# Two more chunks of the MLP's first product inside the last attention slots, in place of zero matmuls, and the rows of two batches transposed earlier

## The chip, the cores and the metric

The kernel runs on one core of a Trainium2 chip. The core has a matrix engine (TensorE, called PE in the profile; its weight loads are shown as PEld), a vector engine (VectorE, DVE), an activation engine (ScalarE, ACT), a general engine (GpSimd, POOL) and a queue engine that issues the transfers (SyncE, SP). Each engine runs its own instructions in order and waits for others by semaphores. The metric is the device time of one execution in microseconds; the median of several runs is compared.

## The reference

One transformer block with two attentions and an MLP, in float32: 16 batches of 256 tokens with 256 features, 16 heads of 16.

```python
x_norm = modulate(_ln(x), shift_a, scale_a)
qkv = x_norm @ W_qkv + b_qkv                       # self-attention, 16 heads
x = x + gate_a[:, None] * (softmax(q k^T * scale) v @ W_proj + b_proj)
q_c = _ln(x) @ W_qc + b_qc                         # attention to the context
kv_c = _ln(context) @ W_kvc + b_kvc
x = x + (softmax(q_c k_c^T * scale) v_c @ W_cproj + b_cproj)
x_norm2 = modulate(_ln(x), shift_m, scale_m)
h = jax.nn.gelu(x_norm2 @ W_mlp1 + b_mlp1)         # 256 -> 1024
x = x + gate_m[:, None] * (h @ W_mlp2 + b_mlp2)    # 1024 -> 256
```

(The two softmax lines are shortened.) The change lies in the MLP: `x_norm2 @ W_mlp1` is called the first product here, `h @ W_mlp2` the second product.

## The kernel before, in words

**Precision.** Float32 products are made of three products of a faster type: each matrix is split into a high part and a low remainder, and high times high, high times low and low times high are summed in PSUM (`mm3`, `mm3_tok`).

**Slots and beats.** There are 32 attention units: 16 of self-attention ("s") and 16 of attention to the context ("c"), in one order, `units`. The last four units, 28 to 31, are all "c" (batches 12 to 15). A loop runs over slots n = -1 to 31, and each slot over eight beats k = 0 to 7 (`beat(n, k)`). In a beat PE makes the scores of unit n+1 from which DVE takes the row maxima (tile `s`, maxima `mx`), and the transposed scores of unit n (tile `st`), which ACT turns into exponentials (`pt`). In beats 0 and 4 the maxima are transposed (`psm`) and sent by SP as a row (`m`) into the stacked queries `big`, and PE multiplies exponentials and values (`o`, 32 instructions). The rest of a beat is other work of neighbouring units: transposing `o` (`psA`, beats 2 and 6), dividing by the sums (`norm`, DVE, tiles `rc` and `A`), transposing again (`psT_a`, beat 4), the output projection (`psP`, beat 6 of the last slots) and, for earlier slots, the projections of units to come. In slots 30 and 31 there are no units to come, so there is less for PE to do; some of the gaps are filled with matmuls of zeros (`busy`, tile `ps_warm`; the words `d2` and `d3` in the table `SL` are two and three of them).

**The tail.** After slot 31 the MLP of all 16 batches runs, in 64 chunks: four chunks per batch, each of 256 hidden features. A chunk is a first product (12 matmuls into one PSUM bank, tile `ph`, `mlp_first`), two gelus on ACT from the same input (`hf` in full float32, `hh` rounded), their difference on POOL (`hl`, `mlp_gelu`) and a second product (12 matmuls, `mlp_second`, accumulated in the tile `s` or `st`). Iteration i of the tail issues the gelu of chunk i+1, the first product of chunk i+2, and the second product of chunk i-1. A batch b also needs: its rows loaded from DRAM (`mlp_load`, SP, tile `x`), a bias added (`mlp_bias`, POOL), layer-norm statistics (`mlp_stats`, DVE, with a power on POOL, `rs_m`), the normalised rows (`mlp_apply`, DVE, `xn_m`), and their transposes, scaled and split into high and low (`mlp_T`: PE `psT_m`, then DVE `xTf_m`, then `wkch` or `wqch`, then DVE `wkcl` or `wqcl`; these tiles were the context weights before). In the tail the bias, the statistics and `xn_m` of batch b+2 are issued in the iteration of chunk 1 of batch b, and the transposes of batch b+1 in that of chunk 0 of batch b.

**Already inside the slots.** For batches 0, 1 and 2 these steps are issued in the attention slots, at the positions in the table `M`. A position p means slot p // 16 + 31 and beat (p mod 16) // 2, after the beat's own work: -17 is the end of beat 7 of slot 29, 1 is beat 0 of slot 31. The four first products of batch 0 are issued in slot 31 as well (table `H`), and since their gelu comes only in the tail (the activation table is changed once), they are parked: DVE adds the bias of the hidden features and copies the bank into a tile in SBUF (`hk`). The tail then begins with the first products of chunks 4 and 5.

**Order.** The order on PE, DVE, POOL and SP is the order of the program (class `InOrder`); on ACT too, up to iteration 23 of the tail.

**PSUM.** Two tags of two banks each are handed out in turn: "gen" (`LONG`) and "tr" (`SHORT`); a new tile waits until the last reader of the tile two before it in its tag is done. In slot 30 the odd beats' scores use "gen". The tags of SBUF tiles that park chunks are `c` (two buffers), `x1` (five) and, after the change, `xg` (two).

**Weights of the MLP.** They are loaded and split inside slots 23 to 31 (`W1P`, `W2P`): the last two pieces of the first product's weights are split in beats 3 and 5 of slot 29, and those of the second product in beats 2, 4 and 6 of slot 30 and beat 0 of slot 31. The loads of `x` rows and of the second product's weights (`w2_0` to `w2_3`, in slots 28 and 29) share five buffers in turn.

Of the kernel before, what the change touches and what calls it, by code (L numbers as in the profile page):

```python
# [21 lines left out]
def pixart_block(  # L22
# [8 lines left out]
    B, N, H = x.shape  # L31
# [20 lines left out]
                return tc.keep_in_program_order(i) if self.on else i  # L52
            return issue

    E_ = {'M': ((-17, -12, -10, -1, 1), (0, 3, 4, 7, 9), (8, 11, 13, 15)), 'CUT': 8, 'LN': {'s': 'pool', 'c': 'pool', 'q': 'pool'}, 'ON': (1, 1, 1), 'L0': -16, 'L1': 1, 'S0': -7, 'A0': 0, 'T0': 1, 'H': (7, 11, 14, 15), 'S1': 5, 'A1': 7, 'L2': 9, 'T1': 9, 'S2': 32, 'AP': 23, 'DV': (0, 1), 'HP': (1, 0), 'BZ': {}, 'AV': {1: [(1, 2), (1, 3)], 9: [(0, 0), (0, 1)]}, 'AHEAD': (0, 0, 0, 0, 0, 2), 'W1P': [(-9, 1), (-8, 1), (-7, 1), (-6, 1), (-5, 1), (-5, 5), (-4, 1), (-4, 3), (-4, 5), (-3, 1), (-3, 3), (-3, 5), (-2, 1)], 'W2P': [(-4, 7), (-3, 0), (-3, 4), (-3, 6), (-3, 7), (-2, 2), (-2, 4), (-2, 6), (-1, 0), (-1, 1)], 'XP': 1, 'IL': 1, 'MF': 0, 'SH': 4, 'RAMP': 1, 'HA': 1, 'MP': 16, 'W': (7, 1, 0, 0), 'PRE': 'z0qp z0kp load rest ld2 one0 silu b12 brow L0a turn L0b b4 L0d scale T0t sc1 hik lok T0h T0l b4 shift b4 hiq L1a L1b bk loq K0a K0b K0x0 K0x1 K0y0p K0y1p L1d T1t K0l T1h K0l0 K0l1 Q0a Q0m bq Q0h Q0x0 Q0y0p Q0x1 Q0y1p T1l Q0l Q0l0 Q0l1 z1kp z1qp K1a K1b hiv lov Q1a Q1b K1x0 K1x1 K1y0 K1y1 K1l K1l0 K1l1 Q1x0 Q1x1 Q1y0 Q1y1 Q1l Q1l0 Q1l1 L2a L2b L2c V0a V0b bv b5 ld3', 'SL': {(-1, 0): 'V1a', (-1, 1): 'T2t T2h T2p vone z2kp z2qp', (-1, 2): 'V1b', (-1, 3): 'rest', (-1,4): 'M0 rest one1 ld4', (-1, 5): 'K2a L3a', (-1, 6): 'K2m L3b L3p L3c', (-1, 7): 'd3 one2 rest', (0, 0): 'd6 rest', (0, 1): 'rest', (0, 2): 'd3', (0, 4): 'rest', (1, 0): 'rest', (1, 2): 'rest', (1, 4): 'rest', (30, 0): 'd3', (30, 1): 'd2', (30, 2): 'd3', (30, 5): 'd3', (31, 1): 'd2'}}

    PE = InOrder(nc.tensor, True)
    ACT, DVE, POOL, SP = (InOrder(e, True) for e in (nc.scalar, nc.vector, nc.gpsimd, nc.sync))
# [6 lines left out]
    LONG, SHORT = "gen", "tr"  # L65
    ps_turn = [0]

    def ps_gen(name, tag=None):


        if tag is None and ps_turn[0] is not None:
            ps_turn[0] ^= 1
            tag = (SHORT, LONG)[ps_turn[0]]
        tag = tag or SHORT
        return psum.tile([P, 512], F32, tag=tag, name=name, bufs=2)
# [29 lines left out]
    brow = const.tile([32, P], F32, name="brow")  # L105
# [8 lines left out]
    def split(hi, lo, src, eng=POOL, hp=0):  # L114
        (DVE, POOL, ACT)[E_['HP'][hp]].tensor_copy(hi, src) if E_['HP'][hp] < 2 else ACT.copy(hi, src)
        eng.tensor_tensor(lo, src, hi, ALU.subtract)
# [9 lines left out]
    sc1 = const.tile([P, 2, 2, B], F32, name="sc1")  # L126
# [142 lines left out]
    def layernorm(src, name):  # L269
# [83 lines left out]
    def mm3(dst, W, f, xT):  # L353

        n = 0
        for k in range(KC):
            for a, b in ((W[0], xT[0]), (W[0], xT[1]), (W[1], xT[0])):
                PE.matmul(dst, a[:, k, f * P:(f + 1) * P], b[:, k],
                          start=(n == 0), stop=(n == 3 * KC - 1))
                n += 1  # L360
# [335 lines left out]
    M = {}  # L696
# [8 lines left out]
    def mlp_bias(b):  # L705
        POOL.tensor_tensor(M[b].xt, M[b].xt, bc_t(cb), ALU.add)
# [16 lines left out]
    def mlp_T(b):  # L723
# [9 lines left out]
        for f in range(KC):  # L733
            DVE.tensor_scalar(y[:, f], pst[:, f * N:(f + 1) * N], sc1[:, 1, f, b:b + 1],
                              cpT[:, 6 + f, b:b + 1], ALU.mult, ALU.add)
        if b in E_['DV']:
            DVE.tensor_copy(hi, y)
# [6 lines left out]

    NCH = NF // 2

    def mlp_first(b, c, park=None):

        ph = ps_gen(f"ph_{b}_{c}", LONG).rearrange("p (j n) -> p j n", j=2)
        for j in range(2):  # L750
            mm3(ph[:, j], W1, 2 * c + j, M[b].xT)
        if park is not None:
            kept = work.tile([P, 2, N], F32, tag=park[0], name=f"hk_{b}_{c}", bufs=park[1])
            for j in range(2):
                f = BM1 + 2 * c + j
                DVE.tensor_scalar(kept[:, j], ph[:, j], bT[:, f:f + 1], None, ALU.add)
            ph = kept
        M[b].h[c] = ph

    def mlp_gelu(b, c):  # L760
        ph = M[b].h.pop(c)
        hf = work.tile([P, 2, N], F32, tag="pt", name=f"hf_{b}_{c}", bufs=5)
        hh = work.tile([P, 2, N], F32R, tag="qkh", name=f"hh_{b}_{c}", bufs=3)
        hl = work.tile([P, 2, N], F32R, tag="qkl", name=f"hl_{b}_{c}", bufs=3)
        for dst in (hf, hh):
            if b == 0:
                ACT.activation(dst, ph, AF.Gelu_apprx_tanh)
                continue
            for j in range(2):
                f = BM1 + 2 * c + j  # L770
                ACT.activation(dst[:, j], ph[:, j], AF.Gelu_apprx_tanh, bias=bT[:, f:f + 1])
        POOL.tensor_tensor(hl, hf, hh, ALU.subtract)
        M[b].hT[c] = (hh, hl)
# [17 lines left out]

    W1P, W2P = E_['W1P'], E_['W2P']
    W1 = [wself[:, 8 * i:8 * i + 8].rearrange("p (k c) h -> p k (c h)", k=KC) for i in range(2)]
    W2 = [big[2][:, 0], big[2][:, 1]]

    def mlp_w1():

        wf = []
        SP.dma_start(cb, cd[0].partition_broadcast(P))
        for j in range(4):  # L800
            wf.append(stage(W_mlp1, j * H, f"w1_{j}", "x"))
            yield
# [56 lines left out]
    w1, w2, rest = mlp_w1(), mlp_w2(), setup_rest()  # L859
# [58 lines left out]
    for i in range(3):  # L918
        for n, f in (("b", f_b), ("hi", f_hi), ("lo", f_lo)):
            word[n + "qkv"[i]] = lambda f=f, i=i: f(i)  # L920
    for w in E_['PRE'].split():
        word[w]()
    for p, ws in E_['SL'].items():
        at[p] += [word[w] for w in ws.split()]
    ACT.on, POOL.on, SP.on = E_['ON']
    at_end = defaultdict(list)
    def end(p, f, *a):
        at_end[p // 16 - 1, p % 16].append(lambda: f(*a))

    for b, ps in enumerate(E_['M']):  # L930
        for p, f in zip(ps, (mlp_load, mlp_bias, mlp_stats, mlp_apply, mlp_T)):
            end(p, f, b)
    for c, p in enumerate(E_['H']):
        end(p, mlp_first, 0, c, (("c", 2), ("x1", 5))[c // 2])
    def unit(n):
        return units[n] if 0 <= n < nu else None

# [176 lines left out]
                lambda: (o.aT.turn(), o.aT.high()), o.aT.low,  # L1114
                lambda: o.proj(0), lambda: o.proj(1), lambda: (o.end(), o.add(), o.store())])
    chunks = [(b, c) for b in range(B) for c in range(NCH)]
    mlp_first(*chunks[4])
    mlp_gelu(*chunks[0])
    next(pst)()
    mlp_first(*chunks[5])  # L1120
    next(pst)()
    for i, (b, c) in enumerate(chunks):
        ACT.on = i < E_['AP']
        if i + 1 < len(chunks):
            mlp_gelu(*chunks[i + 1])
        if c == 0 and 0 < b < B - 1:
            mlp_T(b + 1)
        if i > 3 and i + 2 < len(chunks):
            mlp_first(*chunks[i + 2])
        if i > 0:  # L1130
            mlp_second(*chunks[i - 1])
        for _, f in zip(range(1), pst):
            f()
        if c == 1 and 2 < b + 2 < B:
            mlp_bias(b + 2)
            mlp_stats(b + 2)
            mlp_apply(b + 2)
        if c == 2:
            mlp_residual(b)
        if c == 3 and b + 3 < B:  # L1140
            mlp_load(b + 3)
# [49 lines left out]
```

## Time and profile before

| | us |
|---|---|
| median of 3 runs | 805.61 |
| lowest and highest | 803.01 and 806.17 |
| the profiled execution | 804.78 |
| its span, first to last instruction | 803.0 |

The span is the time between the first and the last instruction that the profile shows; 1.78 us of the profiled execution lie around it. In the timeline an instruction row gives start, length, engine, line, operation, output and inputs, and in brackets the idle time of the engine before it with what ended it. Lengths of matmuls overlap since they are pipelined; the cost of a group is better read from its start to the start of the next group. All kernel lines carry L51, the line of the helper that issues every instruction, so that rows are told apart by their tiles. Slot 30 lies from 566.9 us on, slot 31 from 586.8 to 607.0, the tail after that.

### The profile page before, as it was taken

How to read it: one execution, taken by the hardware profiler on the slowest of the kernel's cores; microseconds unless marked ns; L12 is line 12 of the kernel's file. 1: busy time of each engine (PE TensorE's matmuls, PEld its weight loads, DVE VectorE, ACT ScalarE, POOL GpSimd, SP SyncE). 2: the span in 40 equal slices, each digit the busy share in tenths (PEclk: the TensorE clock that was granted, in tenths of full speed). 3: DMA queues.
4: the chain of work that ended last, by engine and by line, in shares of the span. 5: the costliest groups of instructions: out<-in, count | busy, mean ns of one | idle time of the engine just before them, and what ended most of it. 6: DMA issues, size and time to landing. Idle time of an engine off the chain costs nothing.

```text
span 803.0 us, 23712 instructions
## 1 busy us (share of the span) xinstructions
PE 781.8 (97%) x9455; PEld 660.3 (82%) x9455; DVE 596.0 (74%) x1063; ACT 584.8 (73%) x1024; POOL 465.4 (58%) x405
## 2 busy tenths in 40 slices
PE   9999999999999999999999999999899999999997
PEld 8677777887887877878788788777669999999997
DVE  4787878888888888878887888777674656666662
ACT  3377887888887888878888788877666666666663
POOL 5745837475564647456364767654446666666653
PEclk9999999999999999999999999999999999999999
DMA  6553444345353444535444454534311322212211
GB/s 189 147 172 95 133 113 123 100 120 146 95 147 104 137 107 123 146 94 146 113 132 130 137 151 120 148 101 129 106 42 42 92 60 60 80 58 62 80 43 51
DMA packets 89938, 87.88 MB, mean 109 GB/s; under 512 B 9506, under 2 KB 85572, under 8 KB 89828
## 3 DMA queue, kind: packets, MB, share of 16 engines
q1 hardware_dynamic: 89364, 85.58, 37.7%
q8 instruction: 75, 1.23, 0.7%
q0 software_dynamic: 192, 0.52, 0.2%
q14 instruction: 35, 0.29, 0.1%
q10 hardware_dynamic: 272, 0.26, 0.1%
HBM read 26.97 MB, written 8.46 MB: 44 GB/s over the span
## 4 chain that ended last, share of the span: by engine, by line
PE 79%; DVE 9%; ACT 4%; POOL 3%; issue 3%; DMA 1%; ACTq 0%; POOLq 0%; SPq 0%
PE s L51 17%; PE o L51 14%; PE ph L51 11%; PE st L51 11%; DVE mx L51 7%; PE ps_qc L51 3%; PE ps_kc L51 3%; PE ps_q L51 3%; ACT pt L51 2%; PE ps_P_s L51 2%; PE ps_v_s L51 2%; PE ps_v_c L51 2%; PE psm L51 2%; PE ps_k L51 1%; PE ps_P_c L51 1%
## 5 line engine op out<-in xcount | busy, mean ns | idle before, releaser
L51 DVE TENSOR_REDUCE mx<-s 128x4 f32<-128x1024 f32 (+1 forms) x267 | 309.2, 1163 | 94.6 <-PE s L51 92.0
L51 ACT ACTIVATE pt<-st 128x1024 f32<-128x1024 f32 x252 | 257.0, 1020 | 40.3 <-PE st L51 34.1
L51 PE MATMUL s<-big 63*128 63x256 f32 (+1 forms) x1024 | 122.1, 309 | 6.5 <-DVE mx L51 3.6
L51 PE MATMUL o<-pt,v 128*32 128x256 f32 x2048 | 123.8, 382 | 0.0
L51 POOL TENSOR_TENSOR hl<-hf,hh 128x512 fp32r<-128x512 f32 x64 | 88.7, 1396 | 55.0 <-ACT hh L51 54.0
L51 PEld LDWEIGHTS s<-big 63*128 63x128 f32 (+1 forms) x1024 | 81.2, 185 | 41.6 <-DVE mx L51 19.0
L51 PE MATMUL st<-big 64*128 64x256 f32 (+1 forms) x1024 | 108.8, 284 | 4.9 <-ACT pt L51 4.9
L51 PEld LDWEIGHTS o<-pt,v 128*32 128x32 f32 x2048 | 60.0, 109 | 40.8
L51 PEld LDWEIGHTS st<-big 64*128 64x128 f32 (+1 forms) x1024 | 82.1, 186 | 9.3 <-ACT pt L51 7.5
L51 ACT ACTIVATE hf<-ph,bT 128x256 f32<-128x256 f32 x120 | 50.6, 474 | 27.8 <-PE ph L51 27.8
L51 ACT COPY oT<-o 128x512 f32<-128x512 f32 x63 | 37.0, 587 | 42.5 <-PE o L51 42.5
L51 ACT ACTIVATE hh<-ph,bT 128x256 fp32r<-128x256 f32 x120 | 50.5, 472 | 23.8 <-PE s L51 12.0
L51 POOL TENSOR_TENSOR xTl_c<-y_c,xTh_c 128x512 fp32r<-128x512 f32 x16 | 20.5, 1282 | 61.6 <-PE s L51 52.3
L51 POOL TENSOR_TENSOR xTl_as<-y_as,xTh_as 128x512 fp32r<-128x512 f32 x16 | 20.5, 1279 | 56.4 <-ACT y_as L51 56.4
L51 PE MATMUL ph<-wqch,wself 128*128 128x256 f32 x256 | 51.8, 285 | 0.0
L51 PE MATMUL ph<-wkch,wself 128*128 128x256 f32 x256 | 51.8, 286 | 0.0
L51 POOL TENSOR_TENSOR xTl_ac<-y_ac,xTh_ac 128x512 fp32r<-128x512 f32 x16 | 20.6, 1284 | 52.8 <-ACT y_ac L51 48.8
L51 PE MATMUL s<-big,hh 128*128 128x256 f32 x256 | 47.4, 282 | 0.0
L51 PE MATMUL st<-big,hh 128*128 128x256 f32 x256 | 47.2, 281 | 0.0
L51 DVE TENSOR_SCALAR xn_m<-x,mv_m,rs_m 128x256 f32<-128x256 f32 x32 | 38.4, 1238 | 11.4 <-POOL rs_m L51 11.4
L51 PEld LDWEIGHTS ph<-wqch,wself 128*128 128x128 f32 x256 | 42.0, 191 | 0.4 <-issue 0.4
L51 PEld LDWEIGHTS ph<-wkch,wself 128*128 128x128 f32 x256 | 41.9, 191 | 0.4
(223 smaller groups left out, 2381.0 us busy)
## 6 DMA issues: line engine op xcount, KB each, us to landing
big<-h_kc SPq DMA_DIRECT2D x64, 128.0 KB
big<-h_qc SPq DMA_DIRECT2D x64, 128.0 KB
big<-h_k SPq DMA_DIRECT2D x62, 128.0 KB
big<-h_q SPq DMA_DIRECT2D x62, 128.0 KB
big<-l_k SPq DMA_DIRECT2D x32, 128.0 KB
big<-l_q SPq DMA_DIRECT2D x32, 128.0 KB
c<-in_ctx_dram SPq DMA_DIRECT2D x16, 256.0 KB
g<-gd SPq DMA_DIRECT2D x16, 256.0 KB
```

The source lines that it names most:

```text
L51: i = f(*a, **k)
```

## The change

The four first products in slot 31 become six first products in slots 30 and 31: chunks 0 and 1 of batch 0 are issued in beats 3 and 5 of slot 30 (into "tr" banks), chunks 2 and 3 in beats 1 and 3 of slot 31, and chunks 0 and 1 of batch 1 in beats 5 and 7 of slot 31. All six are parked. The zeros of beat 5 of slot 30 (three) and of beat 1 of slot 31 (two) go; those of beats 0, 1 and 2 of slot 30 stay. So that the rows are there, all steps of batches 0 and 1 move:

| step | batch 0 before | batch 0 after | batch 1 before | batch 1 after |
|---|---|---|---|---|
| load | slot 29 beat 7 | slot 29 beat 1 | slot 31 beat 0 | slot 30 beat 2 |
| bias | slot 30 beat 2 | slot 29 beat 2 | slot 31 beat 1 | slot 30 beat 4 |
| statistics | slot 30 beat 3 | slot 29 beat 3 | slot 31 beat 2 | slot 30 beat 6 |
| normalised rows | slot 30 beat 7 | slot 29 beat 6 | slot 31 beat 3 | slot 31 beat 0 |
| transposes | slot 31 beat 0 | slot 30 beat 1 | slot 31 beat 4 | slot 31 beat 1 |

Batch 2's positions stay. The tail begins with the first products of chunks 6 and 7, and iterations 4 and 5 issue none (before: iterations 0 to 3 none). The gelus of the two parked chunks of batch 1 are issued as one instruction of 512 columns each instead of two of 256 with a bias.

```diff
-'M': ((-17, -12, -10, -1, 1), (0, 3, 4, 7, 9), (8, 11, 13, 15))
+'HT': 'tr', 'M': ((-30, -28, -25, -20, -14), (-11, -7, -3, 0, 2), (8, 11, 13, 15))
...
-'H': (7, 11, 14, 15)
+'H': ((-9, 0, 0, 'x1', 5), (-5, 0, 1, 'xg', 2), (3, 0, 2, 'x1', 5), (7, 0, 3, 'c', 2), (11, 1, 0, 'c', 2), (15, 1, 1, 'xg', 2))
...
-(30, 0): 'd3', (30, 1): 'd2', (30, 2): 'd3', (30, 5): 'd3', (31, 1): 'd2'
+(30, 0): 'd3', (30, 1): 'd2', (30, 2): 'd3'
...
-    def mlp_first(b, c, park=None):
-        ph = ps_gen(f"ph_{b}_{c}", LONG).rearrange("p (j n) -> p j n", j=2)
+    def mlp_first(b, c, park=None, tag=LONG):
+        ph = ps_gen(f"ph_{b}_{c}", tag).rearrange("p (j n) -> p j n", j=2)
...
-            if b == 0:
+            if b == 0 or b == 1 and c < 2:
                 ACT.activation(dst, ph, AF.Gelu_apprx_tanh)
...
-    for c, p in enumerate(E_['H']):
-        end(p, mlp_first, 0, c, (("c", 2), ("x1", 5))[c // 2])
+    for p, b, c, *park in E_['H']:
+        end(p, mlp_first, b, c, park or None, E_['HT'] if p < 0 else LONG)
...
-    mlp_first(*chunks[4])
+    mlp_first(*chunks[6])
...
-    mlp_first(*chunks[5])
+    mlp_first(*chunks[7])
...
-        if i > 3 and i + 2 < len(chunks):
+        if i > 5 and i + 2 < len(chunks):
             mlp_first(*chunks[i + 2])
```

More of the change, by code (lines that the diff above doesn't have):

```diff
@@ L53, in __getattr__ @@
             return issue
-    E_ = {'M': ((-17, -12, -10, -1, 1), (0, 3, 4, 7, 9), (8, 11, 13, 15)), 'CUT': 8, 'LN': {'s': 'pool', 'c': 'pool', 'q': 'pool'}, 'ON': (1, 1, 1), 'L0': -16, 'L1': 1, 'S0': -7, 'A0': 0, 'T0': 1, 'H': (7, 11, 14, 15), 'S1': 5, 'A1': 7, 'L2': 9, 'T1': 9, 'S2': 32, 'AP': 23, 'DV': (0, 1), 'HP': (1, 0), 'BZ': {}, 'AV': {1: [(1, 2), (1, 3)], 9: [(0, 0), (0, 1)]}, 'AHEAD': (0, 0, 0, 0, 0, 2), 'W1P': [(-9, 1), (-8, 1), (-7, 1), (-6, 1), (-5, 1), (-5, 5), (-4, 1), (-4, 3), (-4, 5), (-3, 1), (-3, 3), (-3, 5), (-2, 1)], 'W2P': [(-4, 7), (-3, 0), (-3, 4), (-3, 6), (-3, 7), (-2, 2), (-2, 4), (-2, 6), (-1, 0), (-1, 1)], 'XP': 1, 'IL': 1, 'MF': 0, 'SH': 4, 'RAMP': 1, 'HA': 1, 'MP': 16, 'W': (7, 1, 0, 0), 'PRE': 'z0qp z0kp load rest ld2 one0 silu b12 brow L0a turn L0b b4 L0d scale T0t sc1 hik lok T0h T0l b4 shift b4 hiq L1a L1b bk loq K0a K0b K0x0 K0x1 K0y0p K0y1p L1d T1t K0l T1h K0l0 K0l1 Q0a Q0m bq Q0h Q0x0 Q0y0p Q0x1 Q0y1p T1l Q0l Q0l0 Q0l1 z1kp z1qp K1a K1b hiv lov Q1a Q1b K1x0 K1x1 K1y0 K1y1 K1l K1l0 K1l1 Q1x0 Q1x1 Q1y0 Q1y1 Q1l Q1l0 Q1l1 L2a L2b L2c V0a V0b bv b5 ld3', 'SL': {(-1, 0): 'V1a', (-1, 1): 'T2t T2h T2p vone z2kp z2qp', (-1, 2): 'V1b', (-1, 3): 'rest', (-1,4): 'M0 rest one1 ld4', (-1, 5): 'K2a L3a', (-1, 6): 'K2m L3b L3p L3c', (-1, 7): 'd3 one2 rest', (0, 0): 'd6 rest', (0, 1): 'rest', (0, 2): 'd3', (0, 4): 'rest', (1, 0): 'rest', (1, 2): 'rest', (1, 4): 'rest', (30, 0): 'd3', (30, 1): 'd2', (30, 2): 'd3', (30, 5): 'd3', (31, 1): 'd2'}}
@@ new lines, in pixart_block @@
+    E_ = {'HT': 'tr', 'M': ((-30, -28, -25, -20, -14), (-11, -7, -3, 0, 2), (8, 11, 13, 15)), 'CUT': 8, 'LN': {'s': 'pool', 'c': 'pool', 'q': 'pool'}, 'ON': (1, 1, 1), 'L0': -16, 'L1': 1, 'S0': -7, 'A0': 0, 'T0': 1, 'H': ((-9, 0, 0, 'x1', 5), (-5, 0, 1, 'xg', 2), (3, 0, 2, 'x1', 5), (7, 0, 3, 'c', 2), (11, 1, 0, 'c', 2), (15, 1, 1, 'xg', 2)), 'S1': 5, 'A1': 7, 'L2': 9, 'T1': 9, 'S2': 32, 'AP': 23, 'DV': (0, 1), 'HP': (1, 0), 'BZ': {}, 'AV': {1: [(1, 2), (1, 3)], 9: [(0, 0), (0, 1)]}, 'AHEAD': (0, 0, 0, 0, 0, 2), 'W1P': [(-9, 1), (-8, 1), (-7, 1), (-6, 1), (-5, 1), (-5, 5), (-4, 1), (-4, 3), (-4, 5), (-3, 1), (-3, 3), (-3, 5), (-2, 1)], 'W2P': [(-4, 7), (-3, 0), (-3, 4), (-3, 6), (-3, 7), (-2, 2), (-2, 4), (-2, 6), (-1, 0), (-1, 1)], 'XP': 1, 'IL': 1, 'MF': 0, 'SH': 4, 'RAMP': 1, 'HA': 1, 'MP': 16, 'W': (7, 1, 0, 0), 'PRE': 'z0qp z0kp load rest ld2 one0 silu b12 brow L0a turn L0b b4 L0d scale T0t sc1 hik lok T0h T0l b4 shift b4 hiq L1a L1b bk loq K0a K0b K0x0 K0x1 K0y0p K0y1p L1d T1t K0l T1h K0l0 K0l1 Q0a Q0m bq Q0h Q0x0 Q0y0p Q0x1 Q0y1p T1l Q0l Q0l0 Q0l1 z1kp z1qp K1a K1b hiv lov Q1a Q1b K1x0 K1x1 K1y0 K1y1 K1l K1l0 K1l1 Q1x0 Q1x1 Q1y0 Q1y1 Q1l Q1l0 Q1l1 L2a L2b L2c V0a V0b bv b5 ld3', 'SL': {(-1, 0): 'V1a', (-1, 1): 'T2t T2h T2p vone z2kp z2qp', (-1, 2): 'V1b', (-1, 3): 'rest', (-1,4): 'M0 rest one1 ld4', (-1, 5): 'K2a L3a', (-1, 6): 'K2m L3b L3p L3c', (-1, 7): 'd3 one2 rest', (0, 0): 'd6 rest', (0, 1): 'rest', (0, 2): 'd3', (0, 4): 'rest', (1, 0): 'rest', (1, 2): 'rest', (1, 4): 'rest', (30, 0): 'd3', (30, 1): 'd2', (30, 2): 'd3'}}
```

## The prediction

> **What bounds the kernel now.** I read the page first (busy shares, slices), then the busy time by stage around the change, then the chain of waits, then the timeline of slots 30 and 31 engine by engine. TensorE (PE) is the bound everywhere; the question is where it has gaps.
>
> ```profile
> PE 781.8 (97%) x9455; PEld 660.3 (82%) x9455; DVE 596.0 (74%) x1063; ACT 584.8 (73%) x1024; POOL 465.4 (58%) x405
> ```
>
> By stage (window, its length, then busy us of PE, PEld, DVE, ACT, POOL, granted clock, DMA share, GB/s). The rows are slot 30, slot 31, the head of the tail up to batch 2's transposes, from these to batch 3's, and the rest:
>
> ```profile
> 569.30:587.40 18.10, 15.89 (x173) 11.68 (x165) 13.03 (x27) 11.14 (x15) 9.08 (x9) 1.00 0.21 63
> 587.40:607.00 19.60, 19.34 (x181) 14.33 (x181) 14.11 (x36) 12.35 (x16) 8.95 (x8) 1.00 0.14 43
> 607.00:618.50 11.50, 11.50 (x113) 10.54 (x113) 3.36 (x8) 7.82 (x17) 6.45 (x7) 1.00 0.21 71
> 618.50:630.90 12.40, 12.19 (x104) 11.96 (x102) 7.22 (x14) 8.06 (x20) 9.77 (x8) 1.00 0.32 87
> 630.90:797.00 166.10, 166.10 (x1376) 163.66 (x1377) 97.17 (x180) 102.68 (x244) 100.04 (x79) 1.00 0.21 63
> ```
>
> Slot 30 has 2.2 us without a matmul, slot 31 0.3, the tail only 0.21, at the transposes of batch 3. The reader should see two things: zeros are PE time too (a slot with zeros is full without being useful), and the tail has no slack, so a chunk that leaves it should be worth its 1.43 us. The chain of waits in the tail (start, length) says otherwise:
>
> ```profile
> 618.66 0.44 PE psT_m L51 x4
> 619.10 1.43 PE ph L51 x12
> 620.53 1.43 PE s L51 x12
> 621.97 1.45 PE ph L51 x12
> 623.41 1.49 POOL hl L51
> 624.90 1.25 POOL x L51
> 626.16 1.25 issue
> 627.45 0.70 POOL rs_m L51
> 628.15 0.03 issue
> 628.18 2.67 DVE xn_m L51 x2
> 630.85 0.04 issue
> 630.89 0.55 PE psT_m L51 x3
> ```
>
> Between the transposes of batch 2 (618.50) and of batch 3 (630.89) PE does not set the end: batch 3's bias, statistics and normalising do, 12.3 us after batch 2's transposes. PE fills that time exactly, with two chunks of first product more than the changed kernel will have there. Last, PE in slots 30 and 31: a gap, then the zeros that go, and the price of one chunk (start of ph to the next st):
>
> ```profile
> 577.37 0.50 PE L51 MATMUL st<-big 64*128 64x256 f32 x4 [0.94 <-ACT pt L51]
> 581.13 0.94 PE L51 MATMUL ps_warm<-wz 128*128 128x128 f32 x6
> 590.57 0.71 PE L51 MATMUL ps_warm<-wz 128*128 128x128 f32 x4
> 593.75 0.38 PE L51 MATMUL ph<-wkch,wself 128*128 128x256 f32 x1
> 595.37 0.50 PE L51 MATMUL st<-big 64*128 64x256 f32 x4
> ```
>
> **The change, part by part.** I replay PE from slot 29 to batch 2's transposes in the tail with the trace's own durations and add up its delay there.
>
> *Zeros removed:* d3 of (30,5) from 581.13 to the next s at 582.00, 0.87; d2 of (31,1) from 590.57 to 591.34, 0.77. **-1.64.**
>
> *Chunks.* By the end of slot 31 there are six instead of four; the tail still starts with two. In a slot a chunk takes 593.75 to 595.37, 1.62. **+3.24** before the tail. The parks (DVE, 0.87 each) are costed below. In return the tail's iterations 4 and 5 lose a chunk each, 2 x 1.43 = 2.86.
>
> *The idle 0.94* before st in (30,4), where PE waits for exp: chunk 0 stands just there. **-0.94.** The like gap at 586.82 (1.18) gets nothing put into it and stays.
>
> *Transposes of batches 0 and 1* move from slot 31 to beat 1 of slots 30 and 31; the same 0.58 us each, **0** in the sum. But their DVE work comes in front of other work: xTf 590.32 to 591.35 (1.03), cast 0.46, subtraction 0.65, together 2.14 between the maxima of beats 1 and 2. Then come the maximum of beat 2 (573.91 to 575.05, 1.14) and norm (0.62). xTf starts 0.77 after the transposes (589.55 to 590.32). So A_c is done 0.77+2.14+1.14+0.62 = 4.67 us after the transposes start. Chunk 0 takes the short PSUM buffer ("tr", two, in turn) that psA1 held and norm reads: the order is psT_m0, psA1, d3, ph_0_0. PE reaches it after 0.58 (transposes), 0.38+0.44 (s, st), 0.49 (psA1), 0.76 (d3), 0.34+0.41 (s, st) = 3.40. **+1.27**, a new wait in (30,3). Not seen in the trace of before; it is 0 if the buffers are not taken in turn and 2 if DVE is slowed; psm in 568.91, which waits for the A_c of two tiles earlier, speaks for turns, so I keep 1.27.
>
> *o of (30,4)* takes the buffer of ph_0_0: matmuls, 0.25 to the park, 0.8 of park, so 2.7 after ph starts (599.46 to the park's start at 601.32 is 1.86), while PE arrives after 1.55+0.35+0.42+0.21 = 2.53. **+0.2** (0 to 0.5). psP of (30,6) meets park 1 as it ends: 0. psm at 587.48 waits for DVE now already (0.17); DVE has park 1 and batch 1's statistics more: **+0.1** (0 to 0.9).
>
> *Batch 0's load, bias, statistics, apply* move into slot 29. SP's queue at 555.44 has just issued w2_1; the new load follows. The row at 590.49 shows 2.77 us from issue to the bias that waits for it; behind w2_1's bytes I take 558.7. POOL (idle there) adds the bias, 1.29; the second cut of W1 (558.65) waits behind it, and nobody waits for that before SP's w2_2 load at 564.64. DVE stops in order at the statistics, 560.1 to 561.2 (1.08), and the maximum of beat 4 stands behind them (558.93 before): it ends at 562.34, and s of beat 5 (561.71) needs the bank: 0.7. l_qc and the next maximum run late too, 0.1 more; apply (1.81 beside POOL at 587.25) delays the maximum of beat 7, about 0.05. **+0.85**, from 0.3 (landing at 558.1) to 1.8 (560). SP: batch 0's load no longer stands before the rows of m at 572.71 (0.4 earlier, nobody waits for it). Batch 1's load in (30,2) waits for POOL's cut of w2_0; it issues at about 581, lands at 583.6, and the bias comes before xTl_ac in POOL's queue, which y_ac holds until 586.7 in the replay: 0, up to 1.5 if that load is late. The rows of m behind it on SP are wanted only in slot 31.
>
> Delay at batch 2's transposes: -1.64 + 3.24 - 0.94 + 1.27 + 0.2 + 0.1 + 0.85 = **+3.1**.
>
> *The tail.* hl of chunks 1 to 5 are ready 0.6 us or more before their second product; gelu of chunks 4 and 5 is shorter (1.25 against 1.7). After the transposes of batch 2 PE has left: six products of 1.43, 8.6 us, against 11.5. But the chain above hangs on the same transposes: xTf (+0.71 to +1.71), wkch (+1.8 to +2.8), t_c, gelu of chunk 6 (ACT in order, to +4.8), hl (+4.9), bias, statistics, rs_m, xn_m to +12.3. Nothing in it is removed. Chunk 8's bank is held by chunk 6 until +4.8 too, so PE first waits some 1.6 us there and 1.7 us before batch 3's transposes. The 2.86 us come back as waiting: **0**. Ends: -1.35 if xn_m takes 0.73 as at 596.57 (POOL quiet), 0 if hl of two chunks runs beside it as now, -2.86 if PE alone set the pace. I take 0, the row at the same place. Afterwards the work is the same in both kernels, PE full.
>
> The profiled run took 804.78 (span 803.0 and 1.78 around it); the sum gives 807.9. The median, 805.61, lies 0.8 higher: **808.7**.
>
> [...] The granted clock is 1.00 through every gap here, the longest 1.18 us; the new ones, 1.3 to 1.7, are beyond that. [...]
>
> **The rivals.**
>
> (1) *The tail gives the time back.* For it: PE is busy 166.10 of 166.10 after 630.90. Against it: the chain quoted. Then 3.1 - 2.9 = +0.2: 805.8; without the bank wait -1.0.
>
> (2) *Slower beyond the measurement:* batch 0's rows land late in slot 29. DVE stops in order, and each us of landing after 558.7 is a us of PE. From 559.7 on it decides (+4.1); at 560.3, as if the load waited for all of w2_1's bytes and its own latency, +4.7: 810.3. Against it: SP is free and DMA idle from 558 to 560.
>
> (3) *The chunks are free:* all waits that could be filled are 1.64 of zeros, 0.94, 1.18 and 0.21, together 3.97: 801.6. It needs every new wait to be nothing, so it is nearly out.
>
> **How the numbers follow.** 0.5% is 4.0 us, about what the measurement can tell from no change. Forecast 0.60 (own range 806.8 to 810.6: 0.44 below the bound, 0.16 above); rival 1 0.18; rival 2 0.17; rival 3 0.05, its better half past the bound or near. Faster 0.04, same 0.63, slower 0.33. The range leaves out rival 3 and the worst of rival 2: 804.5 to 811.5.
>
> **What would show it.** Right: a wait of ph on A_c of over 1 us in (30,3); s of (29,5) waiting for mx; PE busy about 9 of 12.3 us between the transposes of batches 2 and 3, with waits of ph on hh and of psT_m on xn_m; these still 12.3 us apart. Wrong: transposes 9 us apart (rival 1), or batch 0's statistics past 561 (rival 2). My sum fails first if DVE's queue in slot 30 runs otherwise than I replayed it.

## The result and the profile after

| | before | after |
|---|---|---|
| median, 6 runs each | 805.03 us | 808.96 us |
| lowest and highest | 802.92 and 806.17 | 806.76 and 810.06 |
| the profiled execution | 804.78 | 808.88 |
| its span | 803.0 | 806.7 |

The ratio is 1.0058, with a 95% interval of 1.0041 to 1.0074: the change makes the kernel slower by 0.58%. (The quotient of the two medians is 1.0049, inside the interval.) The interval lies across the 0.5% that the forecast called about what a measurement can tell. The time forecast was 808.7.

The page of the changed kernel, busy time by engine, first line:

```profile
PE 780.5 (97%) x9445; PEld 658.6 (82%) x9445; DVE 601.6 (75%) x1067; ACT 582.6 (72%) x1020; POOL 465.3 (58%) x405
```

PE does 1.3 us less (five matmuls of zeros, ten records) and the kernel takes 3.7 us of span more, so that PE is idle about 5 us longer. The busy time by stage says where (window, its length, then PE, PEld, DVE, ACT, POOL, granted clock, DMA share, GB/s; the rows are slot 30, slot 31, from the transposes of batch 2 to those of batch 3, and the rest):

```profile
570.70:591.90 21.20, 18.99 (x196) 14.26 (x188) 16.36 (x34) 11.16 (x15) 9.14 (x9) 1.00 0.17 53
591.90:610.10 18.20, 17.91 (x173) 13.32 (x172) 10.53 (x25) 10.86 (x15) 5.45 (x5) 1.00 0.11 33
...
621.60:633.90 12.30, 9.77 (x80) 9.20 (x78) 7.20 (x14) 8.04 (x20) 9.92 (x9) 1.00 0.27 87
633.90:800.70 166.80, 166.00 (x1376) 163.56 (x1377) 97.82 (x180) 101.72 (x242) 100.31 (x79) 1.00 0.23 63
```

Slot 30 became 3.1 us longer with 3.1 us more of PE work and as much idle time as before (2.2). The third row is the one to look at: the stage lasts 12.3 us as before (12.4), but PE works 9.77 of it instead of 12.19. The two products that left the tail left a hole of nearly the same size, 2.53 us of idle time instead of 0.21.

A ledger from the two timelines: the distances between the starts of the products of exponentials and values (o of the first and fifth beat of a slot) and, in the tail, between the transposes (psT_m; where they are split in two rows, the last row). The last column regroups the prediction's own terms.

| stretch | before | after | difference | predicted |
|---|---|---|---|---|
| o (29,0) to o (29,4) | 9.77 | 9.78 | +0.01 | 0 |
| to o (30,0) | 9.86 | 10.97 | +1.11 | +0.85 |
| to o (30,4) | 8.90 | 11.19 | +2.29 | 1.62 - 0.94 + 0.58 + 1.27 + 0.2 = +2.73 |
| to o (31,0) | 9.67 | 10.49 | +0.82 | 1.62 - 0.87 + 0.1 = +0.85 |
| to o (31,4) | 8.12 | 8.78 | +0.66 | 1.62 - 0.77 = +0.85 |
| to o in the tail | 11.23 | 9.12 | -2.11 | -1.62 - 0.58 = -2.20 |
| to batch 2's transposes | 11.47 | 11.47 | 0 | 0 |
| to batch 3's | 12.39 | 12.29 | -0.10 | 0 |
| to batch 4's | 11.85 | 12.92 | +1.07 | 0 |
| to batch 5's | 12.08 | 11.85 | -0.23 | 0 |
| sum | 105.34 | 108.86 | +3.52 | +3.08 |

At batch 2's transposes the delay is +2.78. Batch 4's transposes are one row before and split after, which moves about 0.25 us from one stretch to the next, so that +1.07 and -0.23 are best read together, +0.84. The executions of one kernel spread over 3 to 8 us, so that for small effects these distances say more than the times; both are given below. But a distance comes from one execution.

The waits of PE in the timeline after (start, length, engine, line, operation; in brackets the idle time before and what ended it):

```profile
562.94 0.50 PE L51 MATMUL s<-big 63*128 63x256 f32 x4 [0.86 <-DVE mx L51]
...
581.04 0.28 PE L51 MATMUL psm<-ident,mx 128*16 128x128 f32 x1 [0.52 <-DVE mx L51]
581.72 1.93 PE L51 MATMUL o<-pt,v 128*32 128x256 f32 x32 [0.40 <-ACT m L51]
...
626.32 0.39 PE L51 MATMUL ph<-wkch,wself 128*128 128x256 f32 x1 [1.27 <-ACT hh L51]
...
633.87 0.55 PE L51 MATMUL psT_m<-ident,xn_m 128*128 128x128 f32 x3 [0.88 <-DVE xn_m L51]
...
646.79 0.55 PE L51 MATMUL psT_m<-ident,xn_m 128*128 128x128 f32 x3 [0.80 <-DVE xn_m L51]
```

All are new but the last but one, which was 0.21 in the kernel before. The first is slot 29, the next two slot 30, the last three the tail. With 0.38 more at 632.69, those up to batch 3's transposes are 2.53, which is the idle time of the third window above; the last, 0.80, stands before batch 4's transposes and is nearly all of the +0.84. VectorE in the same execution, and one row of it of the kernel before:

```profile
560.54 0.75 DVE L51 BATCH_NORM_STATS2 st_m<-x 128x6 f32<-128x256 f32 x2 [1.66 <-POOL x L51]
561.67 1.21 DVE L51 TENSOR_REDUCE mx<-s 128x4 f32<-128x1024 f32 x1
...
577.61 1.22 DVE L51 TENSOR_REDUCE mx<-s 128x4 f32<-128x1024 f32 x1
...
579.70 1.28 DVE L51 TENSOR_REDUCE mx<-s 128x2 f32<-128x512 f32 x2
...
633.74 1.77 DVE L51 TENSOR_TENSOR xmg<-x,gm 128x512 f32<-128x512 f32 x1
```

```profile
630.76 0.68 DVE L51 TENSOR_TENSOR xmg<-x,gm 128x512 f32<-128x512 f32 x1
```

The statistics of batch 0 (first row) hold VectorE for 1.66 us until POOL's bias is done, and the maxima that PE's s waits for stand behind them. In slot 30 the maxima of beat 3 end only at 580.98, after the copies of the moved transposes (575.51 to 577.69), the maxima of beat 2 and the norm; psm waits for them. The last row, part of the residual sum of the MLP (`xmg`), takes 1.77 instead of 0.68.

The chain of waits in the tail after:

```profile
622.18 1.43 PE s L51 x12
623.61 1.45 PE st L51 x12
...
626.40 1.49 POOL hl L51
627.89 1.25 POOL x L51
629.15 1.25 issue
...
631.17 2.65 DVE xn_m L51 x2
633.81 1.69 DVE xmg L51
```

It is the chain that the prediction quoted for the kernel before, from hl to xn_m with the same lengths: 1.49, 1.25, 1.25, then 2.65 for xn_m (2.67 before). It goes on one link further, into xmg.

### The profile page after: what moved, and what is told of

Its sections match the earlier page's. It is cut to its first block, busy times and chain, and to the rows that moved or that the text cites. A ratio compares the mean times of both kernels' runs of the same rounds, so it can differ in the third digit from the quotient of the medians.

```text
span 806.7 us, 23693 instructions
## 1 busy us (share of the span) xinstructions
PE 780.5 (97%) x9445; PEld 658.6 (82%) x9445; DVE 601.6 (75%) x1067; ACT 582.6 (72%) x1020; POOL 465.3 (58%) x405
## 4 chain that ended last, share of the span: by engine, by line
PE 74%; DVE 13%; ACT 4%; POOL 4%; issue 3%; DMA 1%; SPq 0%; POOLq 0%; ACTq 0%
PE s L51 15%; PE o L51 13%; PE st L51 11%; PE ph L51 10%; DVE mx L51 8%; PE ps_qc L51 3%; PE ps_q L51 3%; ACT pt L51 3%; PE ps_kc L51 2%; PE ps_P_s L51 2%; PE ps_v_s L51 2%; PE ps_k L51 2%; PE ps_P_c L51 2%; PE psm L51 1%; PE ps_v_c L51 1%
## 5 line engine op out<-in xcount | busy, mean ns | idle before, releaser
L51 ACT ACTIVATE hf<-ph,bT 128x256 f32<-128x256 f32 x116 | 48.7, 473 | 26.9 <-PE ph L51 26.9
L51 ACT ACTIVATE hh<-ph,bT 128x256 fp32r<-128x256 f32 x116 | 48.8, 472 | 23.3 <-PE s L51 11.7
```

What stands on the lines that cost most here:

```text
L51: i = f(*a, **k)
```

## The experiments

Theory: the rows of batches 0 and 1, moved sooner, hold PE by what they ask of VectorE, POOL and the load; the two products taken out of the tail give nothing, since batch 3's rows set the pace there. Rivals: PE's own additional time in the slots is the cost; in the tail a PSUM bank and not the rows; VectorE's order and not its amount of work. Differences below are to the changed kernel or the kernel before, as the edit says. Ratios are always to the kernel before, measured again beside each group of experiments (medians of 803.96 to 805.63), so that the ratios, and not the medians, are to be compared with each other.

**The rows alone.** The kernel before with the changed kernel's positions of the rows; products and zeros stay.

```diff
-'M': ((-17, -12, -10, -1, 1), (0, 3, 4, 7, 9), (8, 11, 13, 15))
+'M': ((-30, -28, -25, -20, -14), (-11, -7, -3, 0, 2), (8, 11, 13, 15))
```

> The kernel before, with only the rows of batches 0 and 1 moved to their new places (load, bias, statistics, normalised rows, transposes); the four chunks, their parks and all zeros as before. Theory rows (the early rows are what delays the slots: the statistics in slot 29 in DVE's order, and batch 0's transposed rows before the maxima of beats 2 and 3 of slot 30): the wait of s for mx in (29,5) and the wait of psm for mx in (30,4) are there without any chunk in slot 30; the tail's first o starts 2.5 to 3 us later than before; with batches 2 and 3 still 12.3 us apart the span is 805.5 to 806.5. Rival chunks (the two added chunks and their PSUM banks cost the time): psm in (30,4) waits no more than before, span 803.0 to 804.3.

Measured: 809.26 us, ratio 1.0057 (1.0040 to 1.0074), the whole of the slowdown. In the ledger +3.28 at batch 2's transposes and +3.32 at batch 5's (the changed kernel +2.78 and +3.52). Two of the waits in its timeline:

```profile
582.31 0.28 PE L51 MATMUL psm<-ident,mx 128*16 128x128 f32 x1 [1.13 <-DVE mx L51]
...
590.04 0.74 PE L51 MATMUL psP_c<-wcph,xTl_ac 128*128 128x256 f32 x4 [1.11 <-POOL xTl_ac L51]
```

The second is POOL's queue: batch 1's bias stands ahead of xTl_ac and waits 2.17 us for its load, the case on which the prediction put 0 to 1.5. In the changed kernel neither is seen at this size: PE reaches both places later because the chunks stand in front, and that load took at most 3.38 us from its issue (581.22) to the bias (584.60), which did not wait for it. So about 1.1 of the 3.28 belong to the load in this execution. With that, the rows alone cost as much as rows and chunks, and two chunks less in the tail bring nothing: with all of them still in the tail, the ledger ends at +3.32.

**PE's time alone.** The kernel before with zeros of a chunk's length where the changed kernel has chunks 0 and 1, and without the two groups of zeros that the change removes.

```diff
-(30, 2): 'd3', (30, 5): 'd3', (31, 1): 'd2'}
+(30, 2): 'd3', (30, 3): 'd6', (30, 5): 'd6'}
```

> The kernel before, with all its rows and products where they are, but with zeros as long as a chunk's first product (twelve of them, 1.74 us by the 0.145 us of each in the six from 581.13 to 582.00) in beats 3 and 5 of slot 30, where the changed kernel has chunks 0 and 1, in place of the three zeros in beat 5 and the two in beat 1 of slot 31. Nothing of the computation is left out or added. This is the TensorE time of the change in slot 30 without its rows, parks and loads. Theory (TensorE time alone, less what stood idle there): from o of (30,0) to o of (30,4) 8.90 + 1.74 - 0.94 = 9.7; from there to o of (31,0) 9.67 as without zeros (st then waits 0.77 for pt) plus 1.74 - 0.77 = 10.6; slot 31's first half 0.77 less, 7.4; sum at the transposes of batch 2 +0.9 over the kernel before, and the time +0.9, ratio 1.001. In the changed kernel the same two distances took 11.19 and 10.49, so that by this theory 1.5 of the first is VectorE's lateness and not TensorE's time. Rival (the exponentials set the pace all through slot 30, as without zeros): 9.0 and 9.7, sum -0.7, ratio 0.999.

Measured: 805.65 us, ratio 1.0012 (0.9996 to 1.0028). The group takes 1.53, from its start to that of s behind it:

```profile
576.98 1.60 PE L51 MATMUL ps_warm<-wz 128*128 128x128 f32 x12
578.51 0.50 PE L51 MATMUL s<-big 63*128 63x256 f32 x4
```

The three distances were 9.41, 10.15 and 7.37 (expected 9.7, 10.6, 7.4; before 8.90, 9.67, 8.12), at batch 2's transposes +0.24. With 1.53 the theory's sum is 2 x 1.53 - 0.94 - 0.77 - 0.77 = +0.6; it is 0.3 too high, but the rival's -0.7 is further off. Against the rows' +3.28 it settles what costs: two chunks of PE time in slot 30, in place of the zeros that go, cost a quarter of a microsecond. The changed kernel's 11.19 in slot 30 is then 9.41 + 0.09 (a chunk is 1.62) + 0.58 (transposes) + 0.52 + 0.40 (its waits for mx and m) = 11.0.

**The load sooner.** The changed kernel with batch 0's load at the end of slot 28.

```diff
-'M': ((-30, -28, -25, -20, -14)
+'M': ((-33, -28, -25, -20, -14)
```

> The changed kernel, with batch 0's rows loaded at the end of slot 28 instead of beat 1 of slot 29; bias, statistics and all else stay. Theory rows: the statistics no longer wait (1.66 us of DVE idle before st_m goes), s in (29,5) doesn't wait for mx, and the tail starts about 1.0 us sooner: span 805.7. Rival: DVE's work and not the landing is the delay in slot 29, then at most 0.3 us are gained, 806.4.

Measured: 807.76 us, ratio 1.0036 (1.0018 to 1.0054). From o of (29,4) to o of (30,0) 10.04 instead of 10.97: 0.93 of the 1.11 in slot 29 is the late load, as expected. (Five profiles with the late load have 10.85 to 11.09 there, the two with the sooner one 10.03 and 10.04.) All other distances stay within 0.01 up to the tail.

**The transposes and chunk 0 later.** Batch 0's transposes leave the place in front of the maxima.

```diff
-'M': ((-30, -28, -25, -20, -14)
+'M': ((-30, -28, -25, -20, -10)
...
-'H': ((-9, 0, 0, 'x1', 5)
+'H': ((-7, 0, 0, 'x1', 5)
```

> The changed kernel with batch 0's four transposes (and the copies of their result behind them) at the end of the fourth beat of slot 30 instead of the last beat of slot 29, and chunk 0's first product at the end of the beat after it, so that both lie in slot 30's second half. Nothing is left out. Theory (VectorE's order): what costs in slot 30 is that VectorE takes 2.9 us of the norm's and the copies' work ahead of the maxima of (30,4), so that psm waits 0.52 us for mx and o 0.40 us for m; with the copies later both waits go, the distance from o of (30,0) to o of (30,4) falls from 11.19 to about 9.0 (chunk 0's 1.62 and some 0.5 of waits leave it) and the next one, to o of (31,0), rises from 10.49 to about 12.1; the sum over both falls by 0.5 to 0.7, and the time by the same, to about 0.9993 of the changed kernel's, ratio to the kernel before 1.005. Rival (TensorE's own work is all of it, the waits only sit in time that it had to spare): the sum over both stays at 21.68 within 0.2, ratio 1.006.

(In this text the earlier place is misnamed: the changed kernel has the transposes at the end of beat 1 of slot 30, not in slot 29.) Measured: 808.54 us, ratio 1.0051 (1.0032 to 1.0069). The waits of psm for mx and of o for m went, as expected, and two others came:

```profile
579.46 1.93 PE L51 MATMUL o<-pt,v 128*32 128x256 f32 x32 [0.26 <-DVE xTf_m L51]
...
584.83 0.39 PE L51 MATMUL ph<-wkch,wself 128*128 128x256 f32 x1 [0.37 <-DVE hk L51]
```

The two distances are 9.23 and 12.74, together 21.97 against 21.68: no gain, 0.3 worse. The theory that the order is at fault falls. VectorE has the rows' work to do in slot 30 in either order, and PE waits for it in one place or the other.

**The zeros that stay.** The changed kernel without the three groups at the start of slot 30.

```diff
-, (30, 0): 'd3', (30, 1): 'd2', (30, 2): 'd3'}
+}
```

> The changed kernel without the zeros left in slot 30 (three in beat 0, two in beat 1, three in beat 2). By the replay: those of beats 0 and 1 are PE time in front of the transposes of batch 0 (0.87 and 0.64), 1.5 us less; those of beat 2 (0.84) lie beside DVE's chain from the transposes of batch 0 to psm of (30,4), which sets that end, so nothing; span 805.2, granted clock unchanged. Rival: the zeros hold the clock, and without them the granted clock falls below 0.99 with the gaps: span over 807.

Measured: 808.1 us, ratio 1.0039 (1.0021 to 1.0056). From o of (30,0) to o of (30,4) 10.31 instead of 11.19: -0.88, where 1.5 was expected. That is the 0.87 of beat 0 alone; the zeros of beats 1 and 2 are worth nothing, and the wait of psm for mx is 1.05 instead of 0.52. VectorE's rows show why (the first two are this run's, the last two the changed kernel's):

```profile
571.90 1.29 DVE L51 TENSOR_REDUCE mx<-s 128x2 f32<-128x512 f32 x2 [1.62 <-PE s L51]
...
578.99 0.86 DVE L51 TENSOR_SCALAR hk<-ph,bT 128x256 f32<-128x256 f32 x2
```

```profile
573.80 1.29 DVE L51 TENSOR_REDUCE mx<-s 128x2 f32<-128x512 f32 x2 [2.48 <-PE s L51]
...
580.89 0.87 DVE L51 TENSOR_SCALAR hk<-ph,bT 128x256 f32<-128x256 f32 x2
```

From the maxima of beat 1 to the end of those that psm waits for (where the park, hk, begins) VectorE has no idle time to speak of and takes 7.09 us in both kernels. So its chain starts at the scores of beat 1, before the transposes of batch 0, and only the zeros ahead of these scores count. That is what the expectation had wrong. The granted clock did not fall (0.9986 on average over the ten executions), against the rival.

**Fewer zeros in the kernel before**, first the two groups that the change removes, then all five of slots 30 and 31.

```diff
-, (30, 5): 'd3', (31, 1): 'd2'}
+}
```

> The kernel before without the two groups of zeros that the change removes, nothing else. The prediction counted them as 1.64 us. Read again, st of (30,6) at 582.38 starts just as exp ends (582.32), so the 0.87 of beat 5 are worth nothing while no chunk stands there, and only the 0.77 of (31,1) go: span 802.2. By the prediction's own term 801.4. If zeros hold the clock: 803 or more.

Measured: 804.09 us, ratio 0.9977 (0.9960 to 0.9994). From o of (30,4) to o of (31,0) 9.69, with zeros 9.67: the group in beat 5 is worth nothing by itself, since st then waits 0.77 for the exponentials. The profiled execution took 806.3 of span all the same, and these stretches of a microsecond show why (columns as above; the granted clock is the third last):

```profile
589.00:590.00 1.00, 0.83 (x9) 0.44 (x13) 1.00 (x2) 0.40 (x2) 0.64 (x1) 0.83 0.00 0
590.00:591.00 1.00, 1.00 (x12) 0.39 (x8) 1.00 (x2) 1.00 (x2) 0.62 (x1) 0.50 0.00 0
591.00:592.00 1.00, 1.00 (x16) 0.53 (x12) 0.43 (x2) 0.05 (x1) 0.43 (x1) 0.50 0.42 151
```

The clock is halved, to 0.50, right behind two waits of 1.18 and 0.17 us, and o of (31,0) takes 3.56 instead of 1.93. Of the other nine executions one has a mean clock of 0.997 too, the rest 0.999 or 1.000.

```diff
-, (30, 0): 'd3', (30, 1): 'd2', (30, 2): 'd3', (30, 5): 'd3', (31, 1): 'd2'}
+}
```

> The kernel before without any zeros in slots 30 and 31. By the replay 0.87 + 0.65 in beats 0 and 1, some 0.4 in beat 2 (then exp is waited for), 0 in beat 5, 0.77 in (31,1): 2.7 us less, span 800.3, granted clock 1.00. Rival: the gaps grow and the clock falls: 803 or more.

Measured: 804.11 us, ratio 0.9982 (0.9965 to 1.0000). At batch 2's transposes -1.72 where -2.7 was expected, at batch 5's 103.64 instead of 105.34; PE's waits for exponentials rise from 3.1 to 4.3 us in the slots. (Its span is the expected 800.3, but by luck: 0.96 of that had been gained before slot 29.) The 0.77 of (31,1) is seen here: from o of (31,0) to o of (31,4) 7.37 instead of 8.12. The o rows of the slots, at 568.20, 575.98, 585.76 and 593.13, take 1.93 each in this execution, so no stretch of low clock met them. That zeros hold the clock isn't shown either way: without two groups its mean is 0.9991, without five 0.9972, in the kernel before beside them 0.9979.

**The bank in the tail.** The changed kernel with chunk 8's first product behind the second product of chunk 5.

```diff
-        if i > 5 and i + 2 < len(chunks):
+        if i > 6 and i + 2 < len(chunks):
             mlp_first(*chunks[i + 2])
         if i > 0:
             mlp_second(*chunks[i - 1])
+        if i == 6:
+            mlp_first(*chunks[i + 2])
```

> The changed kernel, with the first product of chunk 8 issued after instead of before the second product of chunk 5 (iteration 6 of the tail), so that PE need not wait 1.27 us for the bank that chunk 6 holds. Theory rows: batch 3's rows still come 12.3 us after the transposes of batch 2, the wait only moves to the transposes of batch 3, which then wait about 2.5 us; span 806.7 as before this edit, within 0.4. Rival bank (the bank held by chunk 6 is what eats the time given back): 1.2 us less, 805.5.

Measured: 811.46 us, ratio 1.0077 (1.0051 to 1.0102). The wait of ph for hh is gone and batch 3's transposes wait longer instead:

```profile
634.51 0.30 PE L51 MATMUL psT_m<-ident,xn_m 128*128 128x128 f32 x1 [1.76 <-DVE xn_m L51]
635.69 0.55 PE L51 MATMUL psT_m<-ident,xn_m 128*128 128x128 f32 x3 [0.88 <-DVE xn_m L51]
```

1.76 + 0.88 = 2.64, before the edit 1.27 + 0.38 + 0.88 = 2.53; the stage lasts 12.28. The bank only decides where PE waits. (In this execution the granted clock is 0.57, 0.50, 0.50 and 0.72 in the four microseconds from 636 to 640, behind those two waits.)

**Batch 3's rows sooner.** The changed kernel with batch 3's load in iteration 2 of the tail, and its bias (on VectorE) and statistics in iteration 3.

```diff
         if c == 1 and 2 < b + 2 < B:
-            mlp_bias(b + 2)
-            mlp_stats(b + 2)
+            if b > 1:
+                mlp_bias(b + 2)
+                mlp_stats(b + 2)
             mlp_apply(b + 2)
...
+        if i == 2:
+            mlp_load(3)
+        if i == 3:
+            mlp_bias(3, DVE)
+            mlp_stats(3)
-        if c == 3 and b + 3 < B:
+        if c == 3 and 3 < b + 3 < B:
             mlp_load(b + 3)
```

> The changed kernel, with batch 3's rows sooner in the tail: load in iteration 2, bias (on DVE instead of POOL) and statistics in iteration 3, only the normalising still in iteration 5. Theory rows: xn_m of batch 3 is there before PE wants it; the waits of psT_m on xn_m (1.26) go, that of chunk 8 on the bank of chunk 6 (1.27) stays; batch 2's to batch 3's transposes 11.0 instead of 12.3 us; span 805.4, or down to 804.6 if the slow xmg of iteration 6 goes too. Rival bank: nothing changes, 806.7, since the bank's wait is what costs.

Measured: from batch 2's transposes to batch 3's 10.59 instead of 12.29 and to batch 4's 11.91 instead of 12.92; at batch 5's 2.33 less than the changed kernel. (10.59 is to the first of four transposes, 12.29 to the last three; batch 5's are one row in both.) The wait of ph for hh stays, 1.29, as expected; the waits for xn_m are gone:

```profile
631.17 0.60 PE L51 MATMUL psT_m<-ident,xn_m 128*128 128x128 f32 x4
```

This shows that batch 3's rows held the tail. The times don't show it: 809.21 us over five executions from 805.1 to 812.2, ratio 1.0060 (1.0027 to 1.0093), at a mean granted clock of 0.996; the profiled one, at 0.999, took 805.14.

**Both moves in the tail**, the two diffs above in one kernel:

```diff
+        if i == 6:
+            mlp_first(*chunks[i + 2])
...
+        if i == 3:
+            mlp_bias(3, DVE)
+            mlp_stats(3)
```

> The changed kernel with both edits: batch 3's rows sooner, and chunk 8 after the second product of chunk 5. Theory rows: both waits go, batch 2's to batch 3's transposes 9.6 to 10 us, the time given back by the two chunks is seen at last: 2.3 to 2.8 us off, span 804.2 (803.4 with a faster xmg). If the two edits each gave their own wait back alone, the sum would be the same 2.5, so what tells is the other two runs: this one should give more than both single edits together under theory rows (0 and 1.3).

Measured: 807.08 us, ratio 1.0029 (1.0012 to 1.0047). The stage shrinks to 9.18, but the next one takes 14.2: the transposes of the batch behind it wait 0.47 and 0.94 for their own xn_m, and at batch 6's transposes 1.5 us more have passed than with batch 3's rows alone. The expectation missed that: the hole moves to the next batch whose rows weren't moved.

**Four changes together.** Load sooner, transposes and chunk 0 later, no zeros in slot 30, and batch 3's rows sooner with the diff above.

```diff
-'M': ((-30, -28, -25, -20, -14)
+'M': ((-33, -28, -25, -20, -10)
...
-'H': ((-9, 0, 0, 'x1', 5)
+'H': ((-7, 0, 0, 'x1', 5)
...
-, (30, 0): 'd3', (30, 1): 'd2', (30, 2): 'd3'}
+}
```

> The changed kernel with batch 0's load one beat group sooner (end of slot 28), its transposes and chunk 0 later as in the run of that alone, batch 3's rows sooner, and without the three groups of zeros in slot 30. All of the computation is there. If the pieces add: from o of (29,0) to the transposes of batch 2 71.80 - 0.93 (load) - 0.88 (zeros) - 0.6 (order) = 69.4; from there to batch 3's transposes 10.6; to batch 5's transposes 103.6 to 105 instead of 108.86 (105.34 in the kernel before). Ratio to the kernel before 0.996 to 1.000. Rival (what is taken from one stage comes back as a wait in the next, as in the run of both moves in the tail): above 106.0 at batch 5's transposes, ratio 1.002 or more.

Measured: 806.52 us, ratio 1.0022 (1.0008 to 1.0036). At batch 5's transposes 106.67. By the letter these are the rival's signs. The single effects, -0.93, -0.88, +0.29 and -2.33, add up to 108.86 - 3.85 = 105.01. The missing 1.65 is one row of this execution at half the clock (0.50 from 569 to 572), behind waits of 0.94 and 0.35:

```profile
568.71 3.58 PE L51 MATMUL o<-pt,v 128*32 128x256 f32 x32
```

3.58 - 1.93 = 1.65. So but for that row the pieces add in this execution, and what they repair brings the changed kernel back to the kernel before (105.34) and not past it; against the kernel before without zeros in these slots, 103.64, it stays 1.4 behind. The ratio doesn't bear even this out: it is 1.8 us above the kernel before, and the clock doesn't explain that, since its mean over these twelve executions is 0.9989, in the kernel before beside them 0.9981. Where the rest goes isn't shown.

**The kernel before without its five groups of zeros and with batch 3's rows sooner**, two of the edits above:

```diff
-, (30, 0): 'd3', (30, 1): 'd2', (30, 2): 'd3', (30, 5): 'd3', (31, 1): 'd2'}
+}
...
+        if i == 3:
+            mlp_bias(3, DVE)
+            mlp_stats(3)
```

> The kernel before without its five groups of zeros in slots 30 and 31, and with batch 3's rows sooner (load, bias on VectorE and statistics two chunks ahead). All of the computation is there. The kernel before spends 12.39 us from batch 2's transposes to batch 3's, and PE is busy for nearly all of it (its wait there is 0.2), so that the sooner rows can give 0.2 to 0.5: 11.9 to 12.2. From o of (29,0) to batch 5's transposes 103.1 to 103.6 (103.64 without the sooner rows, 105.34 before). Ratio to the kernel before 0.997 to 0.9985. If the chain of batch 3's rows is the bound there too: 11.0 or less for that stage, ratio under 0.997.

Measured: 803.85 us, ratio 0.9979 (0.9962 to 0.9995), the lowest ratio but one, and not told apart from the two with fewer zeros alone. The stage behind batch 2's transposes lasts 11.90 instead of 12.40, the upper edge of the gain that was expected; so in the kernel before PE's work alone takes 11.9 of the 12.4, and the chain sets only the last 0.5. To batch 5's transposes it is 104.68, where 103.1 to 103.6 was expected. Here too one o ran at half the clock (0.50 from 575 to 578), 1.44 longer than 1.93, and without that it is 103.24:

```profile
574.61 3.37 PE L51 MATMUL o<-pt,v 128*32 128x256 f32 x32
```

## Why the prediction was right, and where it wasn't

*The total* was right, +3.1 against 3.9 by the medians. That 808.7 lies so near 808.96 is in part luck: the base, 805.61 from three runs, is 0.58 above the median of six, and the change was put 0.8 too small. By the medians the slowdown is 0.49%, by the ratio 0.58%, on the two sides of the 0.5%. In the ledger 3.08 stands against 3.52: the slots were put 0.30 too high, and the tail, put at 0, costs 0.74 (-0.10, +1.07 and -0.23).

*Why the tail costs.* The step that failed is "Afterwards the work is the same in both kernels, PE full": the work is the same, but PE is not full, since the chain was followed only to xn_m of batch 3. Batch 4's rows come late too, and PE waits 0.80 for them. The timelines show the way there, in us from batch 3's transposes (after, and before in brackets): on VectorE xTf, which stands behind xmg, starts at 1.55 (0.59), wqch on ACT at 2.64 (1.68), hl on POOL behind the next gelus at 5.25 (4.36), and behind that batch 4's bias, statistics and at 10.20 (9.35) its xn_m. It begins with xmg, which takes 1.77 instead of 0.68. In the changed kernel POOL has three hl in a row (631.10 to 634.96) and is in the third when xn_m ends (633.82) and xmg begins; in the kernel before it has two, and is done (630.69) when xmg begins. With batch 3's rows sooner the wait is gone and the stretch is 11.91. The other fifteen xmg of the changed kernel's execution take 0.68 or 0.69. The rows show that xmg and hl ran side by side where xmg took 1.77; that the one slowed the other is the author's reading and isn't shown: at 646.65 xmg takes 0.68 with hl beside it from 646.82 on, and there it is hl that is long, 1.67 where the three in a row take 3.86 together, 1.29 each.

*Slot 29, "+0.85 (0.3 to 1.8)"*: +1.11, of which 0.93 is the load. The statistics start at 560.54, where 560.1 was put (this execution reached slot 29 0.30 later), and s waits 0.86 for mx, the sign that was named.

*The tail, "come back as waiting: 0"*: -0.10. PE waits 1.27 for hh and 0.38 + 0.88 for xn_m, where 1.6 and 1.7 were put, and works 9.77 us where about 9 were expected. The run of the rows alone and the run with batch 3's rows sooner confirm the reason from both sides. This is the part by which rival 1 (the tail gives the time back) is refuted. "PE does not set the end" was too strong for the kernel before, though: with the rows sooner that stage still took 11.90 of 12.40, so PE's work and the chain were nearly equal there, and only the changed kernel is clearly held by the chain. One end of the range given there, -1.35 "if xn_m takes 0.73", doesn't follow from its rows (2.67 - 0.73 = 1.94); it isn't in the sum.

*"A new wait in (30,3), +1.27"* failed. ph of chunk 0 starts at 578.16 with no wait, while norm reads psA only from 578.74: it got another bank than the one the replay gave it. Banks are thus not handed out strictly in turn, as the replay and the description of the kernel before had it; of the prediction's own ends, "0 if the buffers are not taken in turn" is the one that came. VectorE's lateness, which the replay had right, met PE one beat later: 0.52 before psm and 0.40 before o, 0.92 in place of 1.27 and the 0.2 for o. So the sum for this stretch, 2.73 against 2.29, was right for a reason half wrong: the queue was followed to the right engine and the wrong waiter. Its start was wrong too: VectorE is busy without a gap from the maxima of beat 1 on, not from the transposes, as the run without the zeros that stay shows.

*The zeros, "-1.64"*: -0.87 for beat 5 of slot 30 was too much taken alone, where it is worth nothing, and right only because a chunk took the place. Nor are the terms of the sum separate prices in general: the rows alone cost 3.28, PE's time alone 0.24, and both with the removal of the zeros 2.78, less than their sum, because chunks stand where PE would wait for the rows.

*The clock.* The sum without any loss of clock was right for this pair: no stretch of the changed kernel's profile in slots 30 and 31 is below 1.00, and its mean over six executions is 0.9985, against 0.998 for the kernel before in later runs.

*Rival 2* (rows of batch 0 landing past 559.7) did not happen: POOL's bias, which waits for the rows, starts at 559.22; *rival 3* (chunks free) is refuted by the run of the rows alone, though as to PE's time it was nearer than thought: 0.24.

## What to carry to other kernels

Work that is pulled forward into a gap brings its whole chain of preparation with it; price that chain on the engines that are in order and nearly full (here 2 us of copies on VectorE and a load), for the matmuls themselves may be nearly free. Before taking work off the busiest engine in a later stage, ask whether that engine sets the end there or merely has just enough to fill it: 12.19 us of work in 12.4 looks like a bound, but beside it stood a chain that takes 12.3, and taking 2.86 of work away gave 0.1. And replay queues for the amount of lateness, but trust less the one instruction that the replay says will wait.

## What the runs showed of the hardware

In some executions the granted clock falls to 0.50 for about 3.4 us (3.40 to 3.42 by stretches of a microsecond) behind short idle times of PE: behind 1.18 + 0.17 us (the kernel before without two groups of zeros), 0.94 + 0.35 (four changes together), 0.52 + 0.16 + 0.94 within four (the last experiment) and 1.76 + 0.88 (the bank in the tail), each time with matmuls before and between; in the first three one o then takes 3.4 to 3.6 us instead of 1.93. In the run of the rows alone it fell for 6.8 us at 55 us, around waits of 0.64 and 0.20, and in the run of the bank also for 3.4 us at 56 us, around 0.48 and 0.22. The same waits at the same place leave the clock at 1.00 in other executions (the changed kernel has 0.94 + 0.37 there without a loss, and the kernel before without five groups of zeros 0.52 + 0.16 + 0.94), so what decides it isn't shown; the rows of o that it met took 1.4 to 1.7 us longer. An estimate: by a mean granted clock of 0.998 in the kernel before, with 0.5 x 3.4 / 805 = 0.0021 for each stretch, an execution has at most about one of them, in either kernel (their profiles also show a lower clock after the last matmul, from about 802.3 to the end in the kernel before and from about 805.3 in the changed one); by this estimate part of the spread between executions is this.
